# Carried sums, bf16 rests and the residual of attention moved from VectorE to TensorE and ScalarE; mask and log weights on parts of the array; group norm's end in five pieces

## The chip, the cores and the metric

The kernel runs on one core of a Trainium2 chip. The metric is the device time of one execution in microseconds. The engines are TensorE (PE; its weight loads are PEld), VectorE (DVE), ScalarE (ACT), GpSimd (POOL) and SyncE (SP), which only issues transfers. Each takes its instructions in the order of its own queue. "Line n" is a line of the kernel before; nearly all instructions are recorded through one helper (line 31), so groups are told apart by the names of their tiles.

## The reference

An image tensor of 16 x 128 x 64 x 64 passes two layers and an expert layer, with a residual around each:

```python
x = x + conv(_gn(x), ...)            # group norm over 32 groups, then a selective scan (Mamba)
t = tokens(x)                        # 16 x 4096 x 128
t = t + attn(_ln_t(t), W_kv, q_proj)
t = t + ffn(_ln_t(t), ...)           # 64 experts, each takes 8 tokens per image

# conv: xz = u @ W_in; xc = silu(conv4(xs)); dt, B, C = split(xc @ W_xproj)
#       delta = softplus(dt @ W_dt + b); A = -exp(A_log)
#       h = exp(delta*A)*h + delta*xc*B  (16 states);  y = sum(h*C) + xc*D;  out = (y*silu(z)) @ W_out
# attn: kv = silu(x @ W_kv) for 8 heads;  s = q . k
#       m = cummax(s); e = exp(s - m); u = cumsum(e); w = cumsum(e*v);  out = mean over heads of w/u
```

## The kernel before, in words

The first stage, where the change lies, works in blocks of 512 tokens; an image has 8 blocks (`NBLK`), 16 images have 128 (`NK`). One loop over `k` (line 674) interleaves two pieces of work by a hand-written order: the scan layer of block `k` (`cur`), with the ends of block `k-1` (`prev`) and the start of block `k+1` (`nxt`), and attention of block `m = k - 9` (`m`), of `m - 1` (`mp_`) and the layer norm of `m + 1` (`mn`). Each pass of the loop has 16 steps, one for each state `n` of the scan. In a step, VectorE makes `bx` (`product`), `beside(n)` puts the pieces of other work that belong to that step into the queues, `decays` has ScalarE make two `da` tiles for later steps (8 ahead at most), `load_bc` fetches `bct` three steps ahead, VectorE scans the two halves (`scan`, with `between(n)` between them), GpSimd multiplies `h` by C into `da`, and TensorE adds the product of two steps earlier into `y_ps` by transposing it (`add_y`). So the last two products of a block are added in steps 0 and 1 of the next pass. Everything is kept in program order (`InOrder`), so the source's order is the queues' order.

PSUM is the tight resource. `bank` takes one of three banks (pool `ps`) in turn as they come free, and nearly all products share these: `k_ps`, `v_ps`, `w_ps`, `xs_ps`, `o_ps`, `cen_ps`, `dt_ps`, `carry_ps`, `et_ps`, `gn_ps`. One bank (`acc`) serves the scores `s_ps` and attention's output `ao_ps` by turns; `y_ps` and `bx` have their own.

Attention of a block goes through these functions:

- `key`, `score`: silu of eight key projections, scores of 8 heads x 4 chunks in rows of one 128 x 128 tile.
- `score_max`, `score_less`, `score_exp`, `score_sum`, `score_log`: running maximum, weights and sums; `x2` holds the maximum less the score and the log of the sum.
- `score_log` rounds `x2` to bf16 (`parts` 0); `split_more` (VectorE, three instructions on 128 x 256) takes the rests to bf16 twice (`parts` 1 and 2). `store_parts` and `spread_parts` carry them through memory into rows of `lh` and `rh`.
- `weights(m, c)`, for chunk `c` of 128 tokens: log weights as a bf16 product of `lh` and `rh` on top of the causal mask (a product of `identb` and `maskb`), for two halves `u` of the heads, in one bank each; then `exp` to `wm`. The 128 x 512 products use all rows of the array, with zeros in half of `lh[u]`.
- `attend(m, c)`: `ao_ps` over the heads, and `carry_ps`, the chunk's weighted sum of values, in four columns of tiles. `carry_on` (VectorE) adds it to the sum carried from the chunk before; `attend_before` adds the carried sum's part to `ao_ps`.
- `finish(m, half)` (VectorE): output / 8 + residual `xs`, and its store.

A block takes part of attention in two passes: chunks 0 and 1 in steps 12 to 15, chunks 2 and 3 in steps 3 to 8 of the next pass, and `finish` of the first half in step 1 of it, of the second in step 8.

The scan layer's output `o_ps` of a block is added to the image's residual in the tile `res` by a product with `ident` and copied back by ScalarE (`put_back`); only for block 0, for which the residual is not there yet, it is set aside and added by VectorE later (`set_aside`, `add_aside`). `load_residual` runs in steps 8 to 11 of block 1. `gn_end` turns an image's statistics into scale and shift, with two small products through PSUM, all at the end of step 15 of block 6.

Of the kernel before, what the change touches and what calls it, by code (L numbers as in the profile page):

```python
# [39 lines left out]
def conv_attn_hybrid(ctx: ExitStack, tc: tile.TileContext, x, w_in, conv_w, conv_b, w_xproj, w_dt, b_dt,  # L40
# [40 lines left out]
    with ExitStack() as st:  # L81
# [10 lines left out]
        identb = wp.tile([P, P], BF16, name="identb")  # L92
        nc.vector.tensor_copy(identb, ident)
        maskb = wp.tile([P, P], BF16, name="maskb")
# [28 lines left out]
        lh = [wp.tile([P, L], BF16, name=f"lh{u}") for u in range(2)]  # L123
# [10 lines left out]
        nc.vector.memset(carry, 0.0)  # L134
        for u in range(2):
            nc.vector.memset(lh[u], 0.0)
            nc.vector.tensor_reduce(negc, ident[:, 64 * u + 12 : 64 * u + 15], mybir.AxisListType.X, ALU.add)
            nc.vector.tensor_scalar(lh[u], lh[u], negc, None, ALU.subtract)
# [23 lines left out]
        with tc.tile_pool(name="prep", bufs=1) as prep:  # L162
# [4 lines left out]
            nc.vector.tensor_copy(maskb, mask)  # L167
# [63 lines left out]
        def gn_end(b):  # L231
            mv = stp.tile([P, 2], F32, tag="mv", name="mv")
            DVE.bn_aggr(mv, gn[b]["stats"].rearrange("p a b -> p (a b)"))
            gp = bank("gn_ps")
            PE.matmul(gp[:, 0:1], gmat, mv[:, 0:1], start=True, stop=True)
            gs = stp.tile([P, 4], F32, tag="gs", name="gs")
            DVE.tensor_copy(gs[:, 0:1], gp[:, 0:1])
            DVE.tensor_tensor(gs[:, 1:2], mv[:, 0:1], gs[:, 0:1], ALU.subtract)
            DVE.tensor_tensor(gs[:, 1:2], gs[:, 1:2], gs[:, 1:2], ALU.mult)
            DVE.tensor_tensor(gs[:, 1:2], gs[:, 1:2], mv[:, 1:2], ALU.add)  # L240
            gp2 = bank("gn_ps2")
            PE.matmul(gp2[:, 0:1], gmat, gs[:, 1:2], start=True, stop=True)
            ACT.activation(gs[:, 2:3], gp2[:, 0:1], AF.Ln, bias=eps)
            ACT.activation(gs[:, 3:4], gs[:, 2:3], AF.Exp, scale=-0.5)
            DVE.tensor_scalar(gs[:, 1:2], gs[:, 0:1], gs[:, 3:4], -1.0, ALU.mult, ALU.mult)
            gn[b]["gs"] = gs
# [13 lines left out]
        def norm_block(k):  # L260
            w = blocks[k]
            t, gs = w["xb"], gn[w["b"]]["gs"]
            t = t[:, KC - 1 :] if w["i"] == 0 else t
            ACT.activation(t, t, AF.Identity, bias=gs[:, 1:2], scale=gs[:, 3:4])
# [135 lines left out]
        def out_proj(k):  # L400

            w = blocks[k]
            w["o"] = bank("o_ps")
            for a in range(NH2):
                PE.matmul(w["o"], wo[:, a, :], w["z"][:, a, :], start=(a == 0), stop=(a == NH2 - 1 and w["i"] == 0))
            if w["i"]:
                PE.matmul(w["o"].rearrange("p (j i) -> p j i", j=L // HH), ident, tokens_of(w), start=False, stop=True)
# [8 lines left out]

        def set_aside(k):
            w = blocks[k]
            o = short("o")
            ACT.copy(o, w["o"])  # L420
            w["o"] = o

        def add_aside(k):
            w = blocks.pop(k)
            xv = tokens_of(w)
            DVE.tensor_tensor(xv, xv, w["o"].rearrange("p (j i) -> p j i", j=L // HH), ALU.add)
# [123 lines left out]
        def split_more(m):  # L550
            s = att[m]
            x, parts = s.pop("x2"), s["parts"]
            DVE.tensor_tensor(x, x, parts[:, 0], ALU.subtract)
            DVE.tensor_copy(parts[:, 1], x)
            DVE.tensor_tensor(parts[:, 2], x, parts[:, 1], ALU.subtract)
# [6 lines left out]
        def spread_parts(m):  # L562
            s = att[m]
            pd = s.pop("pd").rearrange("p t w s -> t w p s")
            for u in range(2):
                for x in range(4):
                    r = 64 * u + 32 * (x // 2) + 5 * (x % 2)
                    SP.dma_start(lh[u][64 * u + 3 * x : 64 * u + 3 * x + 3, :].rearrange("t (c s) -> t c s", s=P),
                                 pd[:, 0, r : r + CB, :])
                    SP.dma_start(rh[64 * u + 12 : 64 * u + 15, x, :].rearrange("t (c s) -> t c s", s=P),  # L570
                                 pd[:, 1, r : r + CB, :])
# [11 lines left out]
        def weights(m, c):  # L583

            s = att[m]
            wm = s["wm", c] = a1.tile([P, 2, 2, 2, P], F32, tag="wm", name="wm", bufs=2)
            for u in range(2):
                rp = bank("w_ps")
                PE.matmul(rp, identb, bc(maskb.unsqueeze(1), [P, 4, P]), start=True, stop=False)
                PE.matmul(rp, lh[u][:, bass.ts(c, P)], rh[:, :, bass.ts(c, P)],  # L590
                          start=False, stop=True)
                ACT.activation(wm[:, u].rearrange("p q g t -> p (q g t)"), rp, AF.Exp)

        def attend(m, c):


            s = att[m]
            if c % 2 == 0:
                s["o"] = acc.tile([P, L], F32, tag="acc", name="ao_ps")
            cols, v, wm = bass.ts(c % 2, P), s.pop(("v", c)), s.pop(("wm", c))  # L600
            for h in range(HD):
                g, j = divmod(h, 4)

                PE.matmul(s["o"][:, cols], v[:, h, :], wm[:, j // 2, j % 2, g, :], start=(c % 2 == 0 and h == 0),
                          stop=(h == HD - 1), skip_group_check=True)
            cp = s["cp", c] = bank("carry_ps")
            for g in range(2):
                for j in range(4):
                    PE.matmul(cp[32 * j : 32 * j + 32, :P], e1[:, 4 * c + j, g, :], v[:, 4 * g + j, :],
                              start=(g == 0), stop=(g == 1))  # L610

        def carry_on(m, c):

            s = att[m]
            cp = s.pop(("cp", c))
            if m % NBLK == 0 and c == 0:
                DVE.tensor_copy(carry[:, 0, :], cp[:, :P])
            else:
                DVE.tensor_tensor(carry[:, c, :], carry[:, (c - 1) % 4, :], cp[:, :P], ALU.add)
# [6 lines left out]

        def finish(m, half):
# [3 lines left out]
            DVE.scalar_tensor_tensor(xs, s["o"][:, : L // 2], 1.0 / HD, xs, ALU.mult, ALU.add)  # L631
# [25 lines left out]
        gn_load(1, 0)  # L657
        gn_stats(1, 0)
# [3 lines left out]
        gn_end(0)  # L662
# [13 lines left out]
        for k in range(NK + LAG + 1):  # L676
# [7 lines left out]
            stat = divmod(k + 1 + NBLK, NBLK)  # L684
            stat = stat if stat[0] < NB else None

            def between(n):

                if m is not None:
# [4 lines left out]
                    if n == 8:  # L694
                        split_more(m)
# [3 lines left out]
            def beside(n):  # L699

                if n == 0:
                    if mp_ is not None:
                        attend_before(mp_, 1)
                    if prev is not None:
                        add_y(prev, N - 2)
                    if m is not None:
                        key(m, 0), key(m, 1), key(m, 2)
                if n == 1:
                    if mp_ is not None:
                        finish(mp_, 0)  # L710
                    if prev is not None:
                        add_y(prev, N - 1)
# [3 lines left out]
                    if prev is not None:  # L716
                        take_y(prev)
                    if nxt is not None:
                        norm_block(nxt)
                    if cur is not None:  # L720
                        skip(cur)
                if n == 2:
# [14 lines left out]
                if n == 4:  # L737
# [3 lines left out]
                    if mp_ is not None:  # L741
                        weights(mp_, 2)
                        weights(mp_, 3)
                if n == 5:
                    if mp_ is not None:
                        attend(mp_, 2)
                    if prev is not None:
# [3 lines left out]
                if n == 6:  # L751
                    if mp_ is not None:
                        attend(mp_, 3)
                        attend_before(mp_, 2)
                        carry_on(mp_, 2)
                    if nxt is not None:
                        conv(nxt, 0)
                    if prev is not None:
                        set_aside(prev) if i == 1 else put_back(prev)
                if n == 7:  # L760
                    if mp_ is not None:
                        attend_before(mp_, 3)
                    if nxt is not None:
                        conv(nxt, 1)
                    if m is not None:
                        score_log(m)
                    decays(k, n, 2)
                    if m is not None:
                        inverse(m)
                    if nxt is not None:  # L770
                        conv_silu(nxt)
                    if mp_ is not None:
                        carry_on(mp_, 3)
                if n == 8:
                    if mp_ is not None:
                        finish(mp_, 1)
# [27 lines left out]
                if n == 13:  # L804
                    if mn is not None:
                        ln_apply(mn)
                    if i == 1 and prev is not None:
                        add_aside(prev)
                    if m is not None:
                        weights(m, 1)  # L810
                        attend(m, 0)
                        attend_before(m, 0)
                if n == 14:
                    if m is not None:
                        attend(m, 1)
                        carry_on(m, 0)
                if n == 15:
                    if stat is not None:
                        gn_stats(*stat)
                    if m is not None:  # L820
                        carry_on(m, 1)

            for n in range(N):
                if cur is not None:
                    product(cur, n)
                beside(n)
# [15 lines left out]
                if 8 <= n <= 11 and i == 1 and cur is not None:  # L842
                    load_residual(b, n - 8)
                if n == 8 and m is not None:
                    store_parts(m)
                if n == 10 and m is not None:
                    spread_parts(m)
                if n == 7 and mn is not None:
                    load_x(mn)
                if n == 8 and stat is not None:  # L850
                    gn_load(*stat)
                if n == 10 and k + 2 < NK:
                    load_block(k + 2)
                if n == 12 and m is not None:
                    load_x(m)
                if n == 15 and stat is not None and stat[1] == NBLK - 1:
                    gn_end(stat[0])
# [293 lines left out]
```

## Time and profile before

| | |
|---|---|
| time, median of 3 runs (lowest to highest) | 10676.47 us (10672.24 to 10677.11) |
| the profiled execution, its own time | 10670.12 us |
| its span | 10668.4 us |
| scan and attention loop | from 44 us (first `du`) to about 9810 us |
| last stages (experts and output) | from there to the end |
| busy in the span: TensorE, VectorE, ScalarE, GpSimd | 88%, 87%, 66%, 65% |
| mean granted TensorE clock | 0.931 |

The share of busy time is over the whole span. A block of the loop repeats almost exactly, so it pays to read one block from the timeline. A matmul in fp32 is recorded as two passes: 2048 `k_ps` passes are 1024 products. In the table of waits, "A <- B" is the time in which an engine stood idle before A, ended by B.

### The profile page before, as it was taken

Reading aid. Unit: us, or ns where it says so; the run is one execution under the profiler, and the core shown is the slowest. Engines: PE = TensorE matmul, PEld = TensorE weight load, DVE = VectorE, ACT = ScalarE, POOL = GpSimd, SP = SyncE. Lnnn points to the kernel's source line nnn. Section 1 sums busy time; section 2 is a strip of 40 time slices with the busy share of each in tenths; the row PEclk is TensorE's granted clock in tenths of the full one; section 3 lists DMA queues with packets and bytes.
Section 4 is the critical chain, followed back from the end, with each engine's and each line's share of the span. In section 5 each row is a group of like instructions: output and inputs, shape, how many; then the busy total and the mean of one; then the engine's idle time right before and its main releaser. Section 6 shows DMA issues by size and latency. Waiting matters only on the chain.

```text
span 10668.4 us, 165082 instructions
## 1 busy us (share of the span) xinstructions
PE 9433.2 (88%) x59484; PEld 5912.8 (55%) x59484; DVE 9296.3 (87%) x11184; ACT 7034.1 (66%) x11884; POOL 6977.9 (65%) x3875
## 2 busy tenths in 40 slices
PE   6689999999999998999999998999999999988775
PEld 3455555555555555555555555555555555555652
DVE  8999999999999999999999999999999999941743
ACT  5567677676766776767776676766677766755740
POOL 7877777777777777777777777777777777730000
PEclk7689999999999999999999999999999999999886
DMA  5555555545555555555554555555555555521348
GB/s 146 138 155 139 147 138 149 139 141 144 138 151 137 150 139 151 137 143 143 135 153 133 152 139 150 140 139 147 141 146 139 149 139 146 136 72 41 109 160 348
DMA packets 817668, 1530.51 MB, mean 143 GB/s; under 512 B 88960, under 2 KB 174608, under 8 KB 809680
## 3 DMA queue, kind: packets, MB, share of 16 engines
q1 hardware_dynamic: 808656, 1511.02, 50.2%
q8 instruction: 469, 7.68, 0.3%
q10 hardware_dynamic: 8192, 8.93, 0.2%
q14 instruction: 351, 2.88, 0.1%
HBM read 1368.18 MB, written 151.52 MB: 142 GB/s over the span
## 4 chain that ended last, share of the span: by engine, by line
PE 56%; DVE 16%; ACT 15%; issue 5%; POOL 4%; DMA 4%; SPq 1%; POOLq 0%; ACTq 0%; DVEq 0%
PE y_ps L31 10%; DVE h L31 8%; PE v_ps L31 8%; PE xs_ps L31 7%; PE ao_ps L31 7%; PE k_ps L31 4%; POOL da L31 4%; PE o_ps L31 4%; DVE bx L31 3%; ACT L208 2%; PE dt_ps L31 2%; ACT da L31 2%; PE carry_ps L31 2%; PE dbl_ps L31 2%; PE w_ps L31 2%
## 5 line engine op out<-in xcount | busy, mean ns | idle before, releaser
L31 POOL TENSOR_TENSOR da<-h,bct 128x1024 f32<-128x1024 f32 x2048 | 6597.9, 3222 | 2470.7 <-DVE h L31 1524.4
L31 DVE TENSOR_TENSOR_SCAN h<-da,state,bx 128x512 f32<-128x512 f32 x3584 | 4424.3, 1266 | 101.5 <-DVE bx L31 2.8
L31 PEld LDWEIGHTS y_ps<-ident,da 128*128 128x128 f32 x16384 | 2057.4, 152 | 1318.9 <-POOL da L31 652.6
L31 PE MATMUL y_ps<-ident,da 128*128 128x128 f32 x16384 | 2347.5, 294 | 485.3 <-POOL da L31 485.1
L31 ACT ACTIVATE da<-delta,a_neg 128x512 f32<-128x512 f32 x4096 | 2606.8, 722 | 0.2
L31 DVE TENSOR_TENSOR bx<-du,bct 128x1024 f32<-128x1024 f32 x2048 | 2524.5, 1233 | 72.8 <-DMA bct<-bcs 2.7
L31 ACT ACTIVATE kt<-k_ps 128x512 f32<-128x512 f32 x1024 | 586.6, 602 | 862.8 <-PE k_ps L31 858.1
L31 ACT ACTIVATE v<-v_ps 128x512 f32<-128x512 f32 x1024 | 611.6, 599 | 795.3 <-PE v_ps L31 795.2
L31 PE MATMUL k_ps<-xn,wk 128*128 128x512 f32 x2048 | 1047.1, 648 | 0.0
L31 PE MATMUL v_ps<-wv,xn 128*128 128x512 f32 x2048 | 1000.2, 611 | 6.3 <-ACT xc L31 6.0
L31 PE MATMUL ao_ps<-wm,v 128*128 128x128 f32 x8192 | 1003.1, 276 | 0.0
L31 PEld LDWEIGHTS ao_ps<-wm,v 128*128 128x128 f32 x8192 | 971.2, 193 | 25.6 <-issue 6.2
L31 PE MATMUL xs_ps<-xb,wc 128*128 128x512 f32 x2048 | 924.3, 594 | 1.8 <-issue 1.8
L31 DVE TENSOR_TENSOR_SCAN h<-da,bx 128x512 f32<-128x512 f32 x512 | 601.2, 1207 | 15.4 <-DVE bx L31 0.5
L31 PEld LDWEIGHTS v_ps<-wv,xn 128*128 128x128 f32 x2048 | 338.7, 189 | 475.0 <-issue 308.7
L31 PEld LDWEIGHTS k_ps<-xn,wk 128*128 128x128 f32 x2048 | 389.9, 206 | 377.4 <-issue 346.5
L31 PE MATMUL w_ps<-maskb,identb 128*128 128x512 bf16 x1024 | 411.5, 402 | 187.4 <-ACT wm L31 161.2
L31 PEld LDWEIGHTS xs_ps<-xb,wc 128*128 128x128 f32 x2048 | 370.0, 191 | 372.1 <-issue 372.1
L31 ACT ACTIVATE wm<-w_ps 128x512 f32<-128x512 f32 x1024 | 539.4, 594 | 48.2 <-PE w_ps L31 46.6
L31 ACT ACT_TABLE_LOAD x395 | 506.8, 1283 | 14.1 <-PE v_ps L31 6.7
L31 POOL COPY state<-h 128x2 f32<-128x2 f32 x1792 | 472.8, 264 | 0.0
L31 PE MATMUL w_ps<-rh,lh 128*128 128x512 bf16 x1024 | 410.3, 401 | 52.3 <-DMA rh<-pd 52.0
(185 smaller groups left out, 9710.3 us busy)
## 6 DMA issues: line engine op xcount, KB each, us to landing
bct<-bcs SPq DMA_DIRECT2D x2048, 512.0 KB
xs<-t_d SPq DMA_DIRECT2D x256, 256.0 KB
xs<-in_x_dram SPq DMA_DIRECT2D x128, 256.0 KB
xt<-in_x_dram SPq DMA_DIRECT2D x64, 512.0 KB
t_d<-xt SPq DMA_DIRECT2D x64, 512.0 KB
t_d<-xs SPq DMA_DIRECT2D x256, 128.0 KB
t<-t_d SPq DMA_DIRECT2D x128, 256.0 KB
tc<-t_d SPq DMA_DIRECT2D x16, 2048.0 KB
```

What stands on the lines that cost most here:

```text
L31: return lambda *args, **kw: self.tc.keep_in_program_order(f(*args, **kw))
L208: tc.keep_in_program_order(nc.scalar.preload_act_table_set(EXP_LN))
```

## The change

- `carry_on` becomes a ScalarE copy out of PSUM; the sum carried so far is added by TensorE, as a product of `ident` with `carry` into `carry_ps`.
- `split_more` is replaced by `rest` (TensorE: `ident` x `x2` in fp32 less `minusb` x the bf16 parts, in a bank of its own) and `split` (ScalarE copies it to bf16), twice, in step 7.
- `finish` becomes a ScalarE copy with scale 1/8; the residual is added by TensorE (`add_x`: `8 * ident` x `xs` into `ao_ps`). It moves from steps 1 and 8 to steps 0 and 7.
- `lh` is one tile with half `u` in rows `64 u`; each log weight product takes 64 rows; the mask is two products on 64 x 64 parts of the array, of 256 and 512 columns. Both banks of a chunk are taken before its first product.
- The residual is loaded in steps 10 to 13 of block 0, and block 0 is treated as the others; `set_aside` and `add_aside` go.
- Statistics run one block earlier, and `gn_end` is in five pieces in steps 2, 4, 5, 6 and 7 of block 6.
- In step 1, `add_y` of the last product comes after `key` 3 and 4 and `score(m, 0)`, and `take_y` after `norm_block` and `skip`.

```diff
+        identb[1]: ident with its two column halves exchanged; minusb = -ident (bf16); ident_hd = 8 * ident
-        def gn_end(b):
-            ...
+        def gn_end(b, part):
+            w = gn[b]
+            if part == 0:
+                w["mv"] = stp.tile([P, 2], F32, tag="mv", name="mv")
+                w["gs"] = stp.tile([P, 5], F32, tag="gs", name="gs")
+                DVE.bn_aggr(w["mv"], w["stats"].rearrange("p a b -> p (a b)"))
+            mv, gs = w["mv"], w["gs"]
+            if part == 1:
+                w["gp"] = bank("gn_ps")
+                PE.matmul(w["gp"][:, 0:1], gmat, mv[:, 0:1], start=True, stop=True)
+                ACT.copy(gs[:, 0:1], w["gp"][:, 0:1])
+            if part == 2:
+                DVE.tensor_tensor(gs[:, 1:2], mv[:, 0:1], gs[:, 0:1], ALU.subtract)
+                DVE.scalar_tensor_tensor(gs[:, 1:2], gs[:, 1:2], gs[:, 1:2], mv[:, 1:2], ALU.mult, ALU.add)
+            if part == 3:
+                w["gp"] = bank("gn_ps2")
+                PE.matmul(w["gp"][:, 0:1], gmat, gs[:, 1:2], start=True, stop=True)
+                ACT.activation(gs[:, 2:3], w["gp"][:, 0:1], AF.Ln, bias=eps)
+                ACT.activation(gs[:, 3:4], gs[:, 2:3], AF.Exp, scale=-0.5)
+            if part == 4:
+                DVE.tensor_scalar(gs[:, 4:5], gs[:, 0:1], gs[:, 3:4], -1.0, ALU.mult, ALU.mult)
...
-        def split_more(m):
-            s = att[m]
-            x, parts = s.pop("x2"), s["parts"]
-            DVE.tensor_tensor(x, x, parts[:, 0], ALU.subtract)
-            DVE.tensor_copy(parts[:, 1], x)
-            DVE.tensor_tensor(parts[:, 2], x, parts[:, 1], ALU.subtract)
+        def rest(m, part):
+            s = att[m]
+            if part == 1:
+                s["rest"] = bank("rest_ps")
+                PE.matmul(s["rest"][:, : 2 * P], ident, s["x2"].rearrange("p w s -> p (w s)"), start=True, stop=False)
+            PE.matmul(s["rest"][:, : 2 * P], minusb, s["parts"][:, part - 1].rearrange("p w s -> p (w s)"), start=False,
+                      stop=True, skip_group_check=part > 1)
+
+        def split(m, part):
+            s = att[m]
+            ACT.copy(s["parts"][:, part], s["rest"][:, : 2 * P].rearrange("p (w s) -> p w s", s=P))
...
+            rp = [bank("w_ps") for _ in range(2)]
             for u in range(2):
-                rp = bank("w_ps")
-                PE.matmul(rp, identb, bc(maskb.unsqueeze(1), [P, 4, P]), start=True, stop=False)
-                PE.matmul(rp, lh[u][:, bass.ts(c, P)], rh[:, :, bass.ts(c, P)],
-                          start=False, stop=True)
-                ACT.activation(wm[:, u].rearrange("p q g t -> p (q g t)"), rp, AF.Exp)
+                rows = slice(64 * u, 64 * u + 64)
+                PE.matmul(rp[u], lh[rows, bass.ts(c, P)], rh[rows, :, bass.ts(c, P)], start=True, stop=True)
+            for u in range(2):
+                for x in range(2):
+                    at, to = slice(64 * (u ^ x), 64 * (u ^ x) + 64), slice(64 * x, 64 * x + 64)
+                    n = 64 * x + 64
+                    PE.matmul(rp[u].rearrange("p (h t) -> p h t", t=P)[to, :, :n], identb[u][at, to],
+                              bc(maskb[u][at, :n].unsqueeze(1), [64, 4, n]), start=False, stop=True, skip_group_check=True)
+            for u in range(2):
+                ACT.activation(wm[:, u].rearrange("p q g t -> p (q g t)"), rp[u], AF.Exp)
...
+            if not first:
+                PE.matmul(cp[:, :P], ident, carry[:, (c - 1) % 4, :], start=False, stop=True, skip_group_check=True)
         def carry_on(m, c):
-                DVE.tensor_tensor(carry[:, c, :], carry[:, (c - 1) % 4, :], cp[:, :P], ALU.add)
+            ACT.copy(carry[:, c, :], att[m].pop(("cp", c))[:, :P])
...
+        def add_x(m, half):
+            s = att[m]
+            PE.matmul(s["o"][:, : L // 2], ident_hd, s["x"][:, bass.ts(half, L // 2)], start=False, stop=True,
+                      skip_group_check=True)
         def finish(m, half):
-            DVE.scalar_tensor_tensor(xs, s["o"][:, : L // 2], 1.0 / HD, xs, ALU.mult, ALU.add)
+            ACT.activation(xs, s["o"][:, : L // 2], AF.Copy, scale=1.0 / HD)
```

The order of steps 5 to 7 (attention's and the scan layer's pieces as they are queued), before and after:

```
before  5: attend 2, out_proj, score_exp | 6: attend 3, attend_before 2, carry_on 2, conv 0, put_back
        7: attend_before 3, conv 1, score_log, decays, inverse, conv_silu, carry_on 3 | 8: finish 1, ... split_more
after   5: attend 2, carry_on 2, out_proj, score_exp | 6: attend 3, attend_before 2, carry_on 3, conv 0, put_back, gn_end 3
        7: attend_before 3, add_x 1, score_log, rest 1, decays, split 1, conv 1, rest 2, inverse, finish 1, split 2,
           conv_silu, gn_end 4
```

## The prediction

> **What bounds the kernel now.** I read the table of waits first, then the chain that ended last inside two neighbouring blocks (5000 to 5160 us), then ScalarE's timeline in the middle of one block. The waits (us in total, times, longest) name what the change aims at:
>
> ```profile
> PE y_ps L31 <- POOL da L31: 485.1, 301, 6.0
> DVE carry L31 <- PE carry_ps L31: 360.7, 147, 14.6
> PE w_ps L31 <- ACT wm L31: 161.2, 215, 1.6
> ACT gs L31 <- PE gn_ps L31: 129.8, 16, 22.2
> ```
>
> TensorE waits for GpSimd's products and VectorE for the carried sums; group norm's end holds ScalarE for 8.1 us per image (129.8 / 16). The chain says how the first two belong together (start us, us, what):
>
> ```profile
> 5070.43 0.59 PE w_ps L31 x2
> 5071.03 1.78 PE ao_ps L31 x16
> 5072.81 0.62 PE carry_ps L31 x16
> 5073.66 2.46 DVE h L31 x2
> 5076.14 1.23 DVE bx L31
> ...
> 5078.15 1.19 DVE h L31
> 5079.34 1.34 DVE du L31
> 5080.68 1.20 DVE h L31
> 5082.13 3.21 POOL da L31
> 5085.39 1.09 PE y_ps L31 x8
> ```
>
> VectorE stands at `carry_on(m, 0)` until TensorE has the sum at 5073.4, so the scans of steps 14 and 15 are late, GpSimd's last product is late, and TensorE's `add_y` of step 15 starts at 5085.39. The same line stands at 5157.51 in the next block: a period of 72.12 us. The middle of the block is different. There TensorE works without a wait from 5030.7 to 5061, and ScalarE has time in hand:
>
> ```profile
> 5037.77 1.06 ACT L31 COPY xt<-o_ps 128x512 f32<-128x512 f32 x1 [0.99 <-PE o_ps L31]
> 5038.63 2.55 ACT L31 ACTIVATE da<-delta,a_neg 128x512 f32<-128x512 f32 x4
> 5041.09 0.39 ACT L31 ACTIVATE x<-sum,back_sum 128x128 f32<-128x128 f32 x1
> 5041.51 0.41 ACT L31 CAST parts<-x 128x256 bf16<-128x256 f32 x1
> 5041.82 2.56 ACT L31 ACTIVATE da<-delta,a_neg 128x512 f32<-128x512 f32 x4
> 5044.29 1.27 ACT L31 ACTIVATE e<-x,off 128x128 f32<-128x128 f32 x4
> 5045.58 1.28 ACT L31 ACT_TABLE_LOAD   x1
> 5046.87 0.69 ACT L31 ACTIVATE xc<-xs_ps,cb 128x512 f32<-128x512 f32 x1
> 5049.40 0.69 ACT L31 ACTIVATE xc<-xs_ps,cb 128x512 f32<-128x512 f32 x1 [1.84 <-PE xs_ps L31]
> ```
>
> The table for silu is in place at 5046.9, 2.5 us before the second convolution is (5049.4), and ScalarE waits 1.84 us for it.
>
> The starts of `du`, one per block, give the periods: with attention running, blocks 2 to 6 of an image take 72.8 us in the mean, block 0 72.6, block 1 77.6 (`add_aside` waits for the residual's load), block 7 78.5 (group norm's end just before it); 592.9 per image. The undisturbed pattern is 72.1. The 0.7 above it is the clock: in 5012 to 5016 us the granted clock is 0.65 and the four `k_ps` passes after the wait take 3.24 us, 1.72 elsewhere.
>
> VectorE is busy 93% (745 of 800 us from 4800 on), yet it isn't the bound by itself: blocks without attention, where it has nothing between its steps but the gate and `du`, take 64.5.
>
> **What the Trainium skill says.** "TensorEngine Tiling (Array Packing)", Key Properties: tiles work in parallel, but a change of tiling mode drains the array. The trace agrees on column tiles: 16 `carry_ps` passes take 0.57 us where 16 whole-array `ao_ps` passes of as many columns take 1.79. No run here shows row tiles side by side. "TensorE: Matmul & The Clock Gate", What's actually happening: the clock halves after a poorly filled window of about 3.4 us; the 3.24 for 1.72 agrees. "ScalarE: Activation LUTs", What ACT_TABLE_LOAD costs: 186 ns + 0.833 per column without a bias pointer, so 293 for 128 columns and 399 for 256; the trace has 253 (`pls`) and 406 (`parts`).
>
> **The change, part by part** (per block with attention, from the undisturbed 72.1).
>
> 1. End of the block. `carry_on` leaves VectorE: 0.28 us x4 and the 1.66 wait at step 14 go. VectorE then runs from `xn` (5067.5, set by ScalarE's `rstd`, unmoved) through 0.6 + 2.45 + 1.3 + 2.45 + 1.3 + 1.2 + 0.6 + 1.35 + 1.2, to 5080.0 in place of 5081.9. GpSimd is done at 5083.4. `add_y` of 15 also moves behind `key` 3, 4 and `score`. TensorE therefore runs through from `w_ps` at 5070.43 to `yb_ps`: its own work there is 19.0 us (21.85 measured, less 0.5 + 2.06 + 0.3 of waits), plus two `carry` products with the identity (0.22 each, as `ao_ps<-e,carry`) and `add_x` on 256 columns (0.43, half a 512-column pair of passes). 19.8 against 21.85: **-2.1**. What is late next is TensorE itself; 2.7 us of slack on POOL.
>
> 2. Middle of the block. Two more `carry` products: **+0.44**. `add_x(1)` 0.43, the fp32 `rest` 0.43, two bf16 `rest` 0.11 each: **+1.1**, all where TensorE has no gap.
>
> 3. A new wait. `split(2)` stands ahead of silu's table load and needs `rest(2)`, which TensorE has queued behind the second convolution. So the load, 2.5 us early before, now follows it: 0.05 + 0.33 (`split`) + 1.29 (load) + 0.69 (`xc`) = 2.4 us after `rest(2)`. TensorE has `y_ps` 0.87 and `et_ps` 0.11 to do; then `v_ps` needs a bank, and with `rest`, `xs0` and `xs1` in the three, it is xs0's. **+1.4** (0 if a bank is free after all; 2.4 if TensorE has nothing to do meanwhile). That ScalarE is there in time but not earlier: `carry_on(3)`, queued ahead of `put_back` and eight decays, holds it until 5041.6 (idle 4 us before it). It then does 0.86 + 2.46 + 0.42 + 0.31 + 2.47 + 0.33 + 1.29 + 0.33 and stands at `split(2)` at 5050.1; `rest(2)` is done at 5050.7. Decays are made eight steps ahead, so VectorE doesn't wait for them. Behind `finish(1)`, now at 5050 on ScalarE, SyncE holds the store and the load of `bct` 10; VectorE may stall there some 3 to 5 us, covered because it has lost about 4 us of work and waits by then and meets `xn` later anyhow. `load_block` goes ahead of `spread_parts` on SyncE (0.4 us); `weights(m, 0)` needs those 5 us after the last of them was issued (5061.3 to 5067), and moves back by as much as they do.
>
> 4. Mask and log weights. Before, 0.43 us per bank. Packed perfectly a chunk costs 0.43, one after another 1.08 (four of 0.215, two of 0.107). At both places TensorE waits for ScalarE's `wm` to free a bank (0.43 and 0.65), so a saving is hidden; serial running would show as up to +0.43 each. **+0.2** (0 to +0.9 with drains; below nothing only if ScalarE freed the bank sooner, and nothing makes it).
>
> 5. VectorE loses `split_more` (1.1), `finish` (2 x 0.34): nothing on the path, since it meets `xn` with 1.05 us in hand already. Block 0's scans take 1.9 us less than those of other blocks (1207 against 1266 ns, 32 of them), and its period is shorter by 0.2 only: what frees VectorE before `xn` is not paid out.
>
> 6. Clock. The waits at the block's start go (0.7 lost there); the new one, 1.4 us beside transposes, may call it back: **+0.4** (0 to 1.7).
>
> Sum: 72.1 - 2.1 + 0.44 + 1.1 + 1.4 + 0.2 + 0.4 = 73.6 us, +0.8 for an ordinary block.
>
> 7. Once an image. The residual comes a block earlier: block 1's 77.6 becomes an ordinary 73.6, with the identity product (1.7) and `put_back` (1.06 for 0.58) that other blocks have. Its four loads queue on SyncE behind the stores of the same buffer; some 0 to 1 us. Group norm in five pieces: block 7's 78.5 becomes 73.6. Its fourth piece puts `Ln` on ScalarE behind TensorE's whole first convolution: 5042.5 to 5045.4 idle, 0.45 of work, and everything up to `xc` late: +2.5 in block 6.
>
> Image: 8 x 73.6 + 2.5 = 591.3 against 592.9: -1.6, x15 = -24. The first image (no attention) saves 3 in block 1 and 4 in block 7, with the new waits hidden under VectorE: -7. The ten iterations without scans at the end (41 us, TensorE busy 87%) get 2.4 us of products and ping-pong between `rest` and `split`, less VectorE's part: +2 each (0 to 3), +20. Setup (six small casts and a product): +1. Total -10 on the profiled run's 10670.1 (span 10668.4), that is 10660; the median shown is 6 above that run, so about **10670**: no change.
>
> **The rivals.**
> A. Forecast: the trade comes out even. 10670, own range 10580 to 10770 (block +-0.8 x 119). Chance 0.52.
> B. Faster: VectorE is what counts, or the wait of step 3 is covered. For it: 93% busy, and 3.66 us of its work leave (468 us of groups over 128 blocks); against: block 0. Without the 1.4 and the 0.4 a block takes 71.8, an image 577, and -16 x 15 gives 10430. If VectorE's own 69.2 were reached (16 x 3.83 + du, gate, maxima, sums, `xn`, statistics), 10150; I give that little. Chance 0.30.
> C. Slower: row tiles don't overlap and each change of mode drains. Place: the four chunks of `weights`; price 0.43 + 0.43 and half a throttled window, 1.7 x 0.5, on the path, so 75.1 a block: +12 x 15, 10850. It decides once a chunk's six matmuls take over 0.86 us. For it: no row tile in the trace; against: the column tiles. Chance 0.18.
> That the products aren't taken from VectorE at all is excluded by the instruction order.
>
> **How the numbers follow.** A change of 0.2% is 21 us, about what a measurement of this kernel can tell from none. Faster: 0.30 + 0.52 x 0.35; same: 0.52 x 0.2; slower: 0.18 + 0.52 x 0.45. With A's range, C, and B's price without VectorE's floor, the range is 10420 to 10830.
>
> **What would show it.** Right: `carry`, `parts` 1 and 2 and `xs` gone from VectorE; `y_ps <- POOL da` below 100 us; a new wait of `v_ps` for `xc` near 1.4 us x 119; ScalarE waiting for `carry_ps` 3 to 4 us per block; no period of 77 or 78. Wrong: `v_ps` without that wait; VectorE over 95% busy; a `w_ps` chunk over 0.9 us; GpSimd still in TensorE's waits.

## The result, and the profile after

| | before | after |
|---|---|---|
| time, median of 4 runs each on one chip (lowest to highest), us | 10674.35 (10671.52 to 10677.11) | 10784.59 (10780.16 to 10798.17) |
| the profiled execution, its own time, us | 10670.12 | 10798.17 |
| its span, us | 10668.4 | 10796.4 |
| first start of `du` to the last, us | 9327 | 9397 |
| last `du` to the end, us | 1297 | 1354 |
| mean granted TensorE clock | 0.931 | 0.944 |

The changed kernel is slower: ratio 1.0105, 95% interval 1.0088 to 1.0123. Of the 128 us between the two profiled executions, 70 lie between the first and the last `du`, 57 behind the last and under 2 ahead of the first. The forecast for this execution was -10, so 138 are to be explained: the images took 6.8 us more each than forecast (x15, 102), and what follows the last `du` 37 more. The starts of `du` give the mean period of each block of an image (images with attention):

| block | 0 | 1 | 2 | 3 | 4 | 5 | 6 | 7 | image |
|---|---|---|---|---|---|---|---|---|---|
| before | 72.6 | 77.6 | 72.6 | 72.9 | 72.7 | 73.1 | 72.8 | 78.5 | 592.9 |
| after | 81.3 | 72.2 | 73.6 | 74.2 | 73.3 | 73.3 | 76.4 | 73.8 | 598.1 |
| forecast | 73.6 | 73.6 | 73.6 | 73.6 | 73.6 | 73.6 | 76.1 | 73.6 | 591.3 |

Seven columns lie within 1.4 us of the forecast; block 0 is 7.7 us off. The table of waits of the changed kernel (us in total, times, longest):

```profile
ACT carry L31 <- PE carry_ps L31: 796.6, 412, 5.7
...
DVE bx L31 <- DMA bct<-bcs: 477.0, 197, 6.3
...
DVE xn L31 <- ACT rstd L31: 251.1, 90, 19.1
...
PE w_ps L31 <- ACT wm L31: 203.7, 218, 1.5
...
PE v_ps L31 <- ACT xc L31: 175.1, 118, 1.5
...
PE y_ps L31 <- POOL da L31: 165.0, 84, 3.8
...
ACT gs L31 <- PE gn_ps L31: 67.9, 18, 22.4
```

VectorE's wait for the carried sums is gone; ScalarE has it instead, 796.6 us. In a block with attention that is 5.8 us, where 3 to 4 were forecast. TensorE's wait for GpSimd fell from 485.1 to 165.0, and ScalarE's in group norm from 129.8 to 67.9. Two more waits are new. `v_ps <- xc` was forecast (1.4 us x 119; it is 175.1 / 118 = 1.48). `bx <- bct`, 477.0 us, was forecast as covered. The kernel before has

```profile
DVE bx L31 <- DMA bct<-bcs: 2.7, 1, 2.7
```

The chain that ended last, at the same place of a block as in the prediction (start us, us, what):

```profile
4885.91 2.58 PE k_ps L31 x6
4888.48 0.87 PE y_ps L31 x8
4889.36 1.72 PE k_ps L31 x4
4891.07 1.01 PE s_ps L31 x32
4892.09 1.02 PE y_ps L31 x8
4893.11 2.58 PE k_ps L31 x6
4895.69 0.87 PE yb_ps L31 x8
```

TensorE runs from one line into the next, and `k_ps` x4 takes 1.72, the full clock, where it took 3.24. The last product of a block is the `y_ps` behind the scores; nothing of GpSimd is on the chain. In the middle of the block the forecast chain stands as it was described:

```profile
4922.37 0.54 PE rest_ps L31 x3
4922.91 3.44 PE xs_ps L31 x8
4926.50 0.37 ACT parts L31
4926.89 1.28 ACT L31
4928.18 0.69 ACT xc L31
4928.92 1.12 PE v_ps L31 x2
```

`split` 2 (`parts`), silu's table load and the first `xc` are now one after another, and `v_ps` stands behind them.

The 7.7 us of block 0 are on SyncE's timeline (start us, us, engine, line, operation, out<-in):

```profile
4180.69 0.32 SPq L31 DMA_DIRECT2D t_d<-xt  x1
4181.34 0.37 SPq L31 DMA_DIRECT2D bct<-bcs  x1
4189.73 0.33 SPq L31 DMA_DIRECT2D xt<-in_x_dram  x1
4190.12 0.42 SPq L31 DMA_DIRECT2D xb<-in_x_dram  x1
...
4196.98 0.28 SPq L31 DMA_DIRECT2D rh<-pd  x1
4197.36 0.39 SPq L31 DMA_DIRECT2D bct<-bcs  x1
```

The 8 us of nothing between the second line and the third are a wait of the residual's load (`xt<-in_x_dram`) for the store of the same buffer (`t_d<-xt`, the first line). Behind it in the queue stood `load_block`, the sixteen transfers of `lh` and `rh` (to 4196.98) and `bct`, whose distance from the `bct` before it is 16 us. In 4155 to 4240 us the waits are, of SyncE's queue and of VectorE:

```profile
SPq L31 <- ACT xs L31: 13.5, 2, 6.9
SPq L31 <- DMA t_d<-xt: 8.9, 2, 8.0
```

```profile
DVE bx L31 <- DMA bct<-bcs: 12.0, 4, 6.2
```

The first of them is SyncE standing at the stores of attention's output until ScalarE's `finish` is done. VectorE stands 12.0 us for `bct` in this stretch, and TensorE 5.6 us for `rh`.

### The profile page after: what moved, and what is told of

Same layout as the page of the kernel before. It is cut to its first block, busy times and chain, and to the rows that moved or that the text cites. A ratio compares the mean times of both kernels' runs of the same rounds, so it can differ in the third digit from the quotient of the medians.

```text
span 10796.4 us, 171663 instructions
## 1 busy us (share of the span) xinstructions
PE 9656.5 (89%) x62557; PEld 6044.0 (56%) x62557; DVE 9040.8 (84%) x9987; ACT 7270.0 (67%) x12924; POOL 6887.6 (64%) x3875
## 4 chain that ended last, share of the span: by engine, by line
PE 64%; ACT 16%; DVE 8%; DMA 6%; issue 3%; SPq 1%; POOL 1%; DVEq 0%; ACTq 0%; POOLq 0%
PE y_ps L31 11%; PE ao_ps L31 10%; PE v_ps L31 7%; PE k_ps L31 7%; PE xs_ps L31 6%; PE carry_ps L31 4%; ACT da L31 4%; PE o_ps L31 4%; DVE h L31 3%; DVE bx L31 3%; ACT L219 2%; PE s_ps L31 2%; PE dt_ps L31 2%; PE w_ps L31 2%; DMA bct<-bcs 2%
## 5 line engine op out<-in xcount | busy, mean ns | idle before, releaser
L31 POOL TENSOR_TENSOR da<-h,bct 128x1024 f32<-128x1024 f32 x2048 | 6468.7, 3159 | 2633.6 <-DVE h L31 1862.1
L31 DVE TENSOR_TENSOR bx<-du,bct 128x1024 f32<-128x1024 f32 x2048 | 2634.1, 1286 | 541.6 <-DMA bct<-bcs 477.0
L31 PEld LDWEIGHTS y_ps<-ident,da 128*128 128x128 f32 x16384 | 2016.7, 151 | 935.4 <-issue 638.5
L31 PE MATMUL y_ps<-ident,da 128*128 128x128 f32 x16384 | 2314.7, 291 | 165.8 <-POOL da L31 165.0
L31 PE MATMUL v_ps<-wv,xn 128*128 128x512 f32 x2048 | 1026.1, 622 | 203.4 <-ACT xc L31 175.1
L31 PE MATMUL ao_ps<-wm,v 128*128 128x128 f32 x8192 | 1037.3, 281 | 2.7 <-DVE x L31 1.8
L31 PE MATMUL k_ps<-xn,wk 128*128 128x512 f32 x2048 | 943.7, 594 | 0.0
L31 ACT COPY carry<-carry_ps 128x128 f32<-128x128 f32 x512 | 135.4, 264 | 796.6 <-PE carry_ps L31 796.6
L31 PE MATMUL w_ps<-rh,lh 64*128 64x512 bf16 x1024 | 328.5, 418 | 310.2 <-ACT wm L31 203.7
L31 POOL COPY state<-h 128x2 f32<-128x2 f32 x1792 | 511.2, 285 | 0.0
```

The lines of the kernel that those rows point to most:

```text
L31: return lambda *args, **kw: self.tc.keep_in_program_order(f(*args, **kw))
```

## The experiments

They were timed in three groups (1 to 4, 5 to 8, 9 to 11), each on one chip together with the kernel before, whose medians there were 10667.62 to 10673.36. A ratio is against the kernel before of the same group; a difference between two groups carries these few us with it. "Tail" is the time from the last `du` to the end (1297.3 before, 1353.9 after). Where nothing else is said, an edit is to the changed kernel.

**1. The residual loaded two steps later.**

```diff
-                if 10 <= n <= 13 and i == 0 and cur is not None:
-                    load_residual(b, n - 10)
+                if n >= 12 and i == 0 and cur is not None:
+                    load_residual(b, n - 12)
```

> The changed kernel with one edit: the four loads of the next image's residual are queued in steps 12 to 15 of block 0, not 10 to 13. Theory (queue): in block 0 SyncE stands some 8 us at the first of these loads, until the store of the same buffer has landed, and the loads of bct and the 16 small transfers of lh and rh wait behind it; two steps later the store has landed, so block 0 falls from 81.3 to about 73.5 us and the kernel by 15 x 7.7 = 116 us, to about 10670. Rival (bandwidth): stores and loads of 4 MB in one block slow every transfer wherever they are queued; then block 0 stays over 79 us and the kernel over 10750.

Measured: 10719.07 us, 1.0048 [1.0033, 1.0063]; 65.5 below the changed kernel. Block 0 fell from 81.3 to 76.3, the others stayed, the tail was 1344.6. The wait of SyncE's queue for the store of `xt` is what most of block 0's excess came from; not all of it. The forecast of 116 us was too much, and the rival, bandwidth, fell: block 0 is below 79. VectorE's wait for `bct` in block 0 went from 11.3 to 7.4 us.

**2. Silu's table load ahead of `split` 2.**

```diff
-                        split(m, 2)
-                        conv_silu(nxt)
+                        conv_silu(nxt)
+                        split(m, 2)
```

> The changed kernel with one edit: conv_silu (table load and two silu) is queued on ScalarE ahead of split 2, not behind it. Theory: the 1.48 us that TensorE waits at v_ps for xc in every block come from the table load standing behind split 2, which needs rest 2; with the edit the wait falls below 0.5 us and the kernel by about 1.0 us x 119 = 120, to about 10665. Rival (ScalarE is simply late there, held by carry_on 3 and what follows): the wait stays over 1.1 us and the kernel above 10750.

Measured: 10780.35, 1.0102 [1.0085, 1.0118]: no gain. The wait of `v_ps` for `xc` fell from 1.48 to 0.25 us per block, but `et_ps <- xc` (59.0 us in all) and `cen_ps` for the load of `xs` (80.4 us for 32.9) came in its place: 0.38 and 0.57 us per ordinary block. The wait moves, and the block stays at 73.5. The theory was right on the wait and wrong on the time; the rival, ScalarE late in any case, expected the wait to stay.

**3. Log weights and mask on the whole array again**, one bank at a time, as in the kernel before.

```diff
-            rp = [bank("w_ps") for _ in range(2)]
             for u in range(2):
-                rows = slice(64 * u, 64 * u + 64)
-                PE.matmul(rp[u], lh[rows, bass.ts(c, P)], rh[rows, :, bass.ts(c, P)], start=True, stop=True)
-            ... (four mask products a chunk on 64 x 64 parts, then both exps)
+                rp = bank("w_ps")
+                PE.matmul(rp, identb[0], bc(maskb[0].unsqueeze(1), [P, 4, P]), start=True, stop=False)
+                PE.matmul(rp, lh[u][:, bass.ts(c, P)], rh[:, :, bass.ts(c, P)], start=False, stop=True)
+                ACT.activation(wm[:, u].rearrange("p q g t -> p (q g t)"), rp, AF.Exp)
```

> The changed kernel with the mask and log weights of weights() as before (two 128 x 512 products on the whole array for each bank, one bank after the other). Theory: packing is worth nothing, since TensorE waits for ScalarE's wm at both places, and taking both banks first makes it wait longer (0.74 and 1.0 us in place of 0.43 and 0.70); unpacked gives 0 to 0.5 us per block back, 10725 to 10785. Rival (packing pays, row tiles run side by side on the path): unpacked costs up to 0.43 us per chunk, 10785 to 10980.

Measured: 10745.09, 1.0068 [1.0053, 1.0083]: 39.5 us less than with the packed products. Blocks 2 to 7 are shorter by 0.37 us in the mean, the tail by 22. So the packing costs time here, within the 0 to 0.5 us per block expected. Experiment 11 asks why.

**4. The carried sum on VectorE**, at the places that the change gave it, without the product with `ident`.

```diff
-            if not first:
-                PE.matmul(cp[:, :P], ident, carry[:, (c - 1) % 4, :], start=False, stop=True, skip_group_check=True)
...
-            ACT.copy(carry[:, c, :], att[m].pop(("cp", c))[:, :P])
+            DVE.tensor_tensor(carry[:, c, :], carry[:, (c - 1) % 4, :], cp[:, :P], ALU.add)
```

> The changed kernel with the carried sums added by VectorE again (at the new places in the order) and without their product with the identity. Theory: VectorE's late scans are now covered, since add_y of step 15 stands behind key 3, 4 and score; TensorE saves 4 x 0.22 us and ScalarE its four copies and the 4 us of standing at carry_on 3, so 0 to -1.2 us per block, 10640 to 10785. Rival (VectorE's wait for carry_ps was the bound, and taking it away was what kept the change from being worse): +1.5 to 2.2 us per block, 10960 to 11050.

Measured: 11320.27, 1.0611 [1.0596, 1.0627]: 536 us more, 5 per ordinary block (78.4). Its table of waits:

```profile
DVE carry L31 <- PE carry_ps L31: 1303.9, 393, 19.8
...
PE y_ps L31 <- POOL da L31: 543.1, 320, 3.8
...
PE v_ps L31 <- DVE z L31: 181.1, 118, 1.6
```

At the new places, directly behind `attend`, whichever engine makes the sum waits for TensorE. ScalarE stands 5.8 us per block for that, and its copies are on no stretch of the chain shown. VectorE, in the same place, hands the wait on: TensorE waits 378 us more for GpSimd's products (543.1 for 165.0) and 157 more for `z` (181.1 for 23.7), together 4.5 us per block. The four additions of 0.28 us, 1.1 in all, are too short for the 5 us; their place in VectorE's queue is what counts. Both expectations missed; the rival had the direction, and less than half of the size.

**5. The next attention input loaded one step earlier**, on top of 1.

```diff
-                if n == 7 and mn is not None:
+                if n == (6 if i else 7) and mn is not None:
                     load_x(mn)
```

> The kernel with the late residual loads (10719), and the load of the next block's x for the layer norm queued on SyncE one step earlier (step 6), ahead of the store that waits for ScalarE's finish 1; in block 0 it stays at step 7. Theory: in the iterations without scans this load waited behind that store, and cen_ps for the load (3.1 us from issue to landing), which makes them 47.9 us in place of 41; they fall to about 43 and the kernel by 35 to 45, to about 10680. Rival (these iterations are longer by TensorE's added products and by rest and split): less than 15 us.

Measured: 10702.91, 1.0026 [1.0019, 1.0033], 16 below experiment 1, and all of that in the loop (image 591.4 for 593.2). The last seven iterations without scans stayed at 46.9 us (46.5 in experiment 1), so the theory fell. TensorE's wait of 2.3 us at `cen_ps` for the load went, but its waits at `w_ps` for `lh` and `rh` rose from 0.6 to 3.4.

**6. The stores of `finish` queued at the ends of steps 2 and 9**, on top of 5.

```diff
-            SP.dma_start(t2_d[b, :, i * L + half * (L // 2) : ...], xs)     # in finish
+                if n in (2, 9) and mp_ is not None:
+                    store_out(mp_, n // 9)
```

> The kernel of the run beside it, with the stores of finish queued on SyncE two steps after ScalarE's copies (ends of steps 2 and 9), so that SyncE never stands for them. Theory: VectorE's wait for bct (2.9 us per block at step 10) goes, but a block with attention keeps its 73.5 us, since TensorE and ScalarE set it; the kernel within 25 us of that run, block 0 perhaps 2 us shorter. Rival (VectorE's stall there is on the path): 1 to 2.9 us per block, 120 to 340 us off.

Measured: 10665.31, 0.9990 [0.9984, 0.9997]. Block 0 fell from 76.2 to 73.0. VectorE's wait for `bct` fell from 378.5 us (experiment 5) to 4.0 in all, and the ordinary blocks hardly moved (73.3 in the mean of blocks 2 to 5, for 73.6 in the changed kernel): VectorE now waits 639.3 us for `rstd` at `xn` instead of 251.1. That wait was covered, as forecast, everywhere but in block 0, where it fell from 7.0 us to 0.1.

**7. Only what is done once an image**: the kernel *before*, with group norm in five pieces (the fourth ahead of `conv` 0) and the residual loaded in steps 12 to 15 of block 0 and added by TensorE. Attention stays as it was.

> The kernel before, with only what happens once an image: group norm's end in five pieces (the fourth piece ahead of the first convolution), and the residual loaded in steps 12 to 15 of block 0 and added by TensorE in every block. Nothing of attention is changed. Theory: blocks 1 and 7 fall from 77.6 and 78.5 to about 73, block 6 stays near 73, block 0 rises by the 2.7 us that the late loads left; 15 x (4.6 + 5.5 - 2.7) = 110 off, 10555, or 10515 if block 0 doesn't rise. Rival (VectorE fills the time, as it is the bound): less than 50 us off.

Measured: 10566.86, 0.9893 [0.9878, 0.9908]. Block 1 72.4 for 77.6, block 7 73.5 for 78.5, block 6 75.6 for 72.8; image 585.6; tail 1296.8, unchanged. The parts of step 7 are worth 107 us if the load doesn't queue behind the store. Block 6 was expected to stay near 73. There the first convolution, behind the fourth piece, now waits for VectorE's `carry` (23.1 us in 14 of the images), which is some 1.6 of its 2.8 us.

**8. All of it mended**: experiment 6 with the log weights of 3, `conv_silu` ahead of `split` 2 as in 2, and the fourth piece of group norm ahead of `conv` 0.

> The changed kernel with all edits so far together: late residual loads, x load ahead, stores later, weights unpacked, conv_silu ahead of split 2, group norm's fourth piece ahead of the first convolution. Theory: from about 10670 take 0.35 us per block for the weights, 0.5 to 1.0 for silu, now that the load of x is no longer behind finish 1, 2.7 in block 6, 20 in the last iterations: 10450 to 10530. Rival (waits move again, as with silu ahead of split 2 alone): 10600 to 10660.

Measured: **10482.41, 0.9810 [0.9795, 0.9825]**, faster than both kernels. Ordinary blocks 72.25, block 6 72.9, image 578.4, tail 1308.6. Against 7 that is 84 us less: attention's work on TensorE and ScalarE, with its new order, pays once nothing else is lost with it. What each of its parts (carried sums, rests, residual, order of step 1) is worth was not taken apart.

**9 and 10. Experiment 8 in two halves, each on top of 6.** 9 has only the log weights on the whole array; 10 has only the order (`conv_silu` ahead of `split` 2, group norm's piece ahead of `conv` 0), and keeps the packed products.

> Edit: e6_stores_later with only the log weights as in the kernel before (lh of two tiles, whole-array products, one bank at a time); the table load of silu stays behind split 2. It splits what e8_all_mended gained over e6 (-183 us). Theory (the packed weights cost the same wherever the queues stand, 0.3 us per block and some 20 us in the last iterations, as e3 showed): 10665 - 35 - 20 = about 10610, last iterations near 45.3. Rival (the convolution's wait behind split 2 is what binds once the transfers are out of the way, and unpacking only moves TensorE's wait to it): 10640 to 10665. Other rival (unpacking alone makes most of e8): below 10540.

> Edit: e6_stores_later with conv_silu queued ahead of split 2 and gn_end 3 ahead of conv 0; the log weights stay packed (so e8_all_mended without its unpacking). Theory (the order is worth some 0.8 us per ordinary block once no transfer stands behind finish 1, plus 2.2 in block 6, and packing costs what e3 showed): 10665 - 95 - 33 = about 10540, ordinary blocks 72.6, last iterations still near 47. Rival (as in e2 the wait only moves from v_ps to the next products while the packed weights hold two banks at a time): 10630, ordinary blocks 73.3.

Measured: 9 gives 10573.58, 0.9908 [0.9893, 0.9923], that is -92; 10 gives 10577.2, 0.9907 [0.9892, 0.9922], that is -88. Together -180, and 8 has -183: the two add up. 9 came out 36 us below the theory's figure and 34 above that of the rival for which the unpacking makes most of 8: it lies between them, and makes half. 10 came out 37 above the theory and 53 below the rival. So the packing costs more here (92) than in the changed kernel (40), and the order less than I thought (88 for 128). Of the 88 some 20 are the piece of group norm, which experiment 2 did not have: block 6 fell by 1.9 us, the others by 0.57 in the mean. That leaves about 68 for silu's order, worth nothing in experiment 2. In 10 the wait at `cen_ps` that took its place there is down to 1.5 us in all; `et_ps <- xc` (46.6) and `v_ps <- xc` (29.2) are left.

Much of the packing's cost can be read in the iterations without scans at the end. Seven of them, in experiment 10 and then in 8, which differ in the packing alone (window; length; busy time and count of PE, PEld, DVE, ACT and POOL; granted clock; DMA share; GB/s):

```profile
9376.80:9704.20 327.40, 282.48 (x1937) 165.33 (x1935) 24.86 (x98) 176.94 (x337) 0.00 (x0) 0.92 0.07 22
```

```profile
9303.30:9607.00 303.70, 263.65 (x1881) 157.62 (x1880) 24.85 (x98) 176.41 (x338) 0.00 (x0) 0.97 0.07 24
```

One iteration of each, around the same `w_ps` and the 16 `ao_ps` after it, first 10, then 8:

```profile
9573.00:9575.20 2.20, 2.07 (x11) 0.35 (x10) 0.00 (x0) 1.08 (x2) 0.00 (x0) 0.56 0.11 43
9575.20:9579.00 3.80, 3.80 (x22) 3.57 (x24) 0.00 (x0) 1.09 (x2) 0.00 (x0) 0.50 0.00 0
```

```profile
9488.30:9489.90 1.60, 1.53 (x8) 0.82 (x9) 0.00 (x0) 1.12 (x3) 0.00 (x0) 1.00 0.51 164
9489.90:9491.80 1.90, 1.90 (x21) 1.78 (x22) 0.00 (x0) 0.95 (x2) 0.00 (x0) 1.00 0.00 0
```

In both kernels TensorE has just waited some 3 us for `lh` and `rh` (0.73 + 2.61 in 10, 3.14 in 8). At half clock the same 16 `ao_ps` take 3.78 for 1.95 us. But these two iterations are not the rule. In 8 only two of the seven go on at 1.00; in the other five a stretch of 3.41 us at half clock follows the wait, after whole-array products too. In 10 all seven are throttled there, five of them for 6.83 us, and four have another stretch of 3.41 behind the next wait for `wm`. So the difference is one of how much: 7.8 us at half clock per iteration in 10, which costs 3.9, against 2.4 and 1.2 in 8; the iterations take 46.8 and 43.4. The other pairs that differ in the packing alone go the same way: 9.3 against 2.4 us at half clock in 6 and 9, and 6.3 against 3.9 in the changed kernel and 3. "TensorE: Matmul & The Clock Gate" of the Trainium skill, What's actually happening, has the clock at half after an idle window of about 3.4 us; the stretches here are 3.41 and 6.83, one window and two, and the waits ahead of them some 3. Why packed products bring more of them stays open. That the share of the array in use is what the gate counts was not tested by itself, and the waits around the products differ a little between the kernels as well (1.54 us for `wm` in 10, 1.30 in 8).

**11. Both banks taken first, products on the whole array**: experiment 8 with the bank order of the changed kernel.

```diff
+            rp = [bank("w_ps") for _ in range(2)]
             for u in range(2):
-                rp = bank("w_ps")
                 ... (both whole-array products of u into rp[u])
-                ACT.activation(wm[:, u]..., rp, AF.Exp)
+            for u in range(2):
+                ACT.activation(wm[:, u]..., rp[u], AF.Exp)
```

> Edit: e8_all_mended, but weights() takes both of a chunk's banks before its first product and makes both exps after the last, as the changed kernel does; the products stay whole-array (not packed). It tells the packed products from the way the banks are taken. Theory (packing itself saves 0.2 us of TensorE per chunk, and what it costs comes from taking both banks first): slower than e8 by 0.3 us per block or more and by some 20 us in the last iterations: 10535 or above. Rival (row tiles and their changes of mode cost it): as e8, 10482, w_ps waiting no longer than there.

Measured: 10481.12, 0.9820 [0.9803, 0.9836], the same as 8. My theory fell: the order of the banks costs nothing, and the packed products themselves do. In blocks 2 to 5 the packed kernel (10) takes 72.8 us and this one 72.3. TensorE's wait for `wm` is 0.4 us longer in 10 (1.70 for 1.30 per block), and the clock loses 0.2 more (1.56 for 1.39). What the packed products save in busy time comes back as that wait.

## Why the prediction was wrong

It forecast no change at 10670, with 10420 to 10830 as range; it is 10784.6. It came out inside that range but clearly slower, and the forecast was that nothing would change. The ordinary block was read right; two terms, of step 7 and of the last iterations, were not. That the total lies near rival C's 10850 is chance: C's reason, in the ordinary block, isn't where the time went.

**Step 1, right.** -2.1 was forecast from the end of attention's `w_ps` to `yb_ps` (its own figures, 19.86 for 21.85, give 2.0); in those of blocks 2 to 5 where the clock lost nothing there, it went from 21.8 to 19.5, -2.3. In the blocks with attention TensorE's wait for GpSimd went from 322 us in all to 4, so GpSimd is off the path as step 1 had it; the other 161 of the 165.0 in the table lie in the first nine blocks, which have no attention, and which I had left out when I wrote "below 100".

**Steps 2 and 3, right.** From `add_x` 1's place to `v_ps` +2.5 was forecast and +2.7 measured (4.42 to 7.14); the earlier piece, from `attend` 2 to the first convolution, gained 0.45, forecast 0.44.

**Step 4, inside its bounds.** +0.2 (0 to 0.9) was forecast for the packing, with the saving hidden; experiments 3, 9 and 11 show 0.4 to 0.5 per block in the mean of blocks 2 to 7. The two row halves do run at the same time, so the first half of rival C's mechanism isn't there:

```profile
4903.76 0.39 PE L31 MATMUL w_ps<-rh,lh 64*128 64x512 bf16 x2
4904.07 0.41 PE L31 MATMUL w_ps<-maskb,identb 64*64 64x256 bf16 x4
4904.42 0.39 PE L31 MATMUL w_ps<-rh,lh 64*128 64x512 bf16 x1
```

The two products of the first line start 3 ns apart, and a chunk takes 0.66 us (start to start of the next) where two whole-array banks take 0.86. It is below the 0.86 from which C decides. C's second half, a loss at each change of mode, fits the trace but is small: 0.66 is 0.23 more than two products of 0.216, over two changes. What C named beside it, the clock, does come, but mostly in the last iterations.

**Step 5, right.** Experiment 6 took the last 378.5 us of VectorE's waits for `bct` away, and the ordinary blocks didn't pay it out (73.3 in 5 and in 6), although in the changed kernel the chain runs through a load of `bct` a little later in the block (5.36 us from 4944.85). Rival B, "VectorE is what counts", falls with it. (`split_more` and `finish` were read too short: by the groups of the kernel before they take 1.5 and 2 x 0.42 us, not 1.1 and 2 x 0.34. Nothing follows from it.) B's other half, that the wait of step 3 could be had back, is true in part and only after the transfers are mended: ordinary blocks take 72.8 in experiment 10, and 72.25 in 8, without the packing, against the 71.8 that B forecast.

**Step 6, right.** The throttled stretches at the block's start went, and little was called back. In the kernel before, those of blocks 2 to 5 that have no throttled stretch take 72.1 us and all of them 72.8 in the mean; in the changed kernel it is 73.3 and 73.6. So the clock costs 0.3 where it cost 0.7, -0.4; the forecast had -0.7 and +0.4. The other terms come to +1.15 (forecast +1.04), and the sum for an ordinary block, 73.6, is what blocks 2 to 5 take in the mean.

**Step 7, the first failure.** "Its four loads queue on SyncE behind the stores of the same buffer; some 0 to 1 us." It is 7.7 us in block 0 (81.3 for 73.6), x15 = 116 us, as much as the whole slowdown. I had the queue and the store before my eyes and took the wait for the store's landing at next to nothing, without a reason. The load waits for the landing of a store issued 9 us earlier, and everything that SyncE holds behind it waits too: `bct`, three steps ahead of its use, was 16 us after the last. Experiment 1 gave 5.0 of the 7.7 back and experiment 6, which takes SyncE's other wait away, another 3.2. The other terms of step 7 held: block 1 72.2, block 7 73.8, block 6 76.4 (forecast 73.6, 73.6, 76.1).

**The last iterations, the second failure.** "+2 each (0 to 3), +20": measured +57. Seven of them take 46.8 us for 41.3 (views as in experiments 9 and 10; first the kernel before, then the changed one):

```profile
9514.50:9803.50 289.00, 247.17 (x1777) 142.67 (x1773) 46.24 (x161) 162.84 (x281) 0.00 (x0) 0.95 0.08 25
```

```profile
9599.70:9927.40 327.70, 275.83 (x1937) 158.18 (x1935) 24.86 (x98) 177.68 (x337) 0.00 (x0) 0.93 0.08 23
```

That +5.5 an iteration is 1.4 of more waits of TensorE (7.4 for 6.0), 1.2 of clock (3.2 lost for 1.9) and, what is left, 2.9 of products. The products were forecast at 2.4. The waits and the clock were not priced, since I took less of VectorE's work to balance them, and VectorE, busy 46 of 289 us, was never the bound there. The packing is some 22 of the 57 (experiment 3), or about 39 once the transfers are mended (1350.4 to 1311.5 us of tail, 6 to 9). With the whole array 11 of the 57 are left (experiment 8).

## What to carry to other kernels

Before a load is moved, write down what stands in the issuing queue at the new place: a load that waits for a store of the same buffer costs what is left of the store's landing (8 us here, of 9 since its issue) for everything behind it, not the issue of four instructions. What an edit is worth depends on the waits beside it (the packed products cost 40 us in the changed kernel and 92 on top of experiment 6; silu's order brought nothing in experiment 2 and some 68 us in 10), so mend one wait first and measure the next edit on top. A sum that waits for another engine belongs on the engine with time to wait; its length matters less than its place in the queue (0.28 us of addition, 5 us of block).

## What the runs showed of the hardware

Row tiles of 64 rows start 3 ns apart and run together, as "TensorEngine Tiling (Array Packing)" of the Trainium skill, Key Properties, says; the chunk of 0.66 us is two passes of 0.216 with about 0.1 us more at each change between 64 x 128 and 64 x 64 tiles (0.66 - 0.43, over two changes). Saving TensorE's busy time by packing lost time all the same, by the wait for the bank (0.4 us per block) and by the clock (7.8 us at half clock for 2.4 in the last iterations). The first whole-array product behind the column tiles of `carry_ps` costs about 0.1 us more as well: the product with `ident` runs 0.33 us to the start of the next one, and the `ao_ps<-e,carry` behind it 0.22, where in the kernel before `ao_ps<-e,carry` itself stood first and took the 0.33. So the change is paid once, whichever product comes first, and a carried sum on TensorE adds 0.22.
